# Narrower buffer waits between two layers: waits by tile, page buffers at the far end of memory, five blocks loaded ahead

## The chip, the cores and the metric

The kernel runs on one core of one Trainium2 chip. Its engines each work through their own queue of instructions: TensorE (PE, with its weight loads as PEld) multiplies, VectorE (DVE) and ScalarE (ACT) do elementwise work, GpSimd (POOL) here mostly issues indirect transfers (gathers and scatters by a list of rows), and SyncE (SP) issues plain transfers. The metric is the device time of the kernel in microseconds; the number that counts is the median of several runs.

## The reference, cut to what matters

The input x is 128 graphs of 64 nodes with 256 features, 8192 rows ("tokens") in all. Two layers follow each other, and each has a graph part and a mixture of experts:

```python
# layer 0
x = x + L0_gnn(layernorm(x), adj)          # adj @ x, W1 to 1024, rmsnorm, silu, W2 back to 256
x = x + L0_ffn(layernorm(x))               # below
# layer 1
x = x + L1_gnn(layernorm(x), adj)          # layer norm, adj @ h @ W_rel + h @ W_root, relu, residual
x = x + L1_ffn(layernorm(x))               # 8 experts, top 2, hidden width 512

def L0_ffn(x):                             # 64 experts, top 6
    top_logits, indices = top_k(x @ gate_w.T, 6)
    scores = softmax(top_logits)
    xW = einsum('bsd,bskde->bske', x, lattice_weights[indices])   # a 256x256 matrix per choice
    h = x + einsum('bske,bsk->bse', xW, scores) @ out_w.T + out_b
    return layernorm(h) * ln_g + ln_b
```

All data are float32. Each token has six answers from layer 0's experts, and these six are added up before layer 1 can do anything with the token.

## The kernel before, in words

The kernel has four stages, one after the other.

**Layer 0's blocks** (L579 to L791). 32 blocks of 256 tokens go through the graph part and the gate. `place` works out, for each of a token's six choices, a row in a table in DRAM (`r0x`) that is grouped by expert, and `send` (L314, on POOL) scatters the rows there. When block READY-1 is placed, `look_back` (L169) notes how many rows each expert has by then. After the last block `page_table` (L338) makes a list of pages, 128 rows of one expert each: first the first full pages of every expert (up to R = 3), then the other full pages, then the pages with a rest. `page_table` also works out (L383 to L386) whether the first READY blocks have rows that lie beyond their experts' first full pages; if so, the page count is set so high that the conditional tail of pages runs.

**Layer 0's pages** (L794 to L848). 424 pages, in pairs: `fetch` (L457, on SP) loads a page into one of 46 buffers `px`, `flip` transposes it (L817, L819), `apply` multiplies it by its expert's matrix in `lat` (L831) and by the scores (L836, into `px` again), and `reply` (L321, on POOL) scatters the 128 answers out of `px` to `r0y`, ordered by token. 23 more pages stand in a conditional tail (L845); whether they run is read from the page table. The replies of pages 192 (R times 64 experts) and up form a group of their own, "r0last".

**Layer 1's blocks** (L852 to L1063). Again 32 blocks, laid out by `staggered` as a software pipeline: step s runs the stages of several blocks, `load3(s+2)`, `mixture(s+1)`, `layer_out(s)`, the convolution of block s-1 and s-2, and `choose1`, `count1`, `place1` of block s-3. `load3` (L884 on SP) loads the 1536 answers of a block into one of two buffers `y`, and the block's `xn1`, `x1` and adjacency; `mixture` (L901) transposes and adds the six answers on TensorE. `place1` sends the rows to layer 1's table (L314 again, now `r1x`). For the first READY blocks `load3` says that the y load need not wait for the "r0last" replies (L886, L887). The order on PE, DVE and ACT is the order of the code (`manual_schedule`, L490); that on SP and POOL is decided by the scheduler when the kernel is built. `load_w2` (L1034) loads the second weights `fw2` of layer 1's experts in the course of this stage.

**Layer 1's pages** (L1066 to L1141). 69 pages of 256 rows: `fetch1` loads a page and its expert's first weights (`px`, `pw`, `pb2`), `flip1`, `up` (L1110) and `down` (L1130) compute, and `add` (L331, on POOL) adds the result into the output.

**Buffers.** SBUF pools are laid out one after the other. `lat` (128 KB per partition, L559) holds first the working data of layer 0's blocks and then all 64 expert matrices; `wx0` with `px` and `pxT` lies behind it during the page stage. When the page stage is over, both are given up, and the pools `keep` (fw2, 32 KB), `wx1` (layer 1's page buffers, about 41 KB), `c3` (constants, about 9 KB) and `work3` (the blocks' working data, about 82 KB) come into their place, in this order. The first instruction that uses a buffer in memory that an earlier pool has given up has to wait for the earlier users of that memory. By default a pool waits for all users of the memory that it takes over, whichever of its tiles is asked for. PSUM pools work in the same way.

Of the kernel before, what the change touches and what calls it, by code (L numbers as in the profile page):

```python
# [18 lines left out]
PSUM = bass.MemoryType.PSUM  # L19
# [452 lines left out]
def two_layer_gnn_moe_kernel(ctx: ExitStack, tc: tile.TileContext, a: dict, out: bass.AP):  # L472
# [12 lines left out]
    KH = H0 // P  # L485
    K0 = 6
    E1, F1, _ = a["L1_ffn_W2"].shape
    READY = 4
    KF = F1 // P
    ctx.enter_context(tc.manual_schedule(engines={ENG.PE, ENG.DVE, ENG.Activation}))  # L490

# [87 lines left out]
    with tc.tile_pool(name="c0", bufs=1) as c0, \  # L579
# [161 lines left out]
        def place(b):  # L741
            B = blocks[b]
            r0.normalize(*B["w"], B["xs"])
            r0.send(r0.places(b, B["hot"]), B["xs"])
            if b == READY - 1:
                r0.look_back()
# [44 lines left out]
            nc.sync.dma_start(out=lat[:, e:e + EB], in_=lat_w[:, e:e + EB])  # L791


    with tc.tile_pool(name="wx0", bufs=3) as wx, \  # L794
            tc.tile_pool(name="pt1", bufs=4, space=PSUM) as pt_pool, \
            tc.tile_pool(name="py1", bufs=4, space=PSUM) as py_pool:
        npair = (r0.pages + 1) // 2
        pairs = [dict() for _ in range(npair)]
        regs = {}

        def fetch(j):
            Q = pairs[j]
            for q in range(2):
                i = 2 * j + q
                if i % 4 == 0:
                    regs["row"] = r0.load(0, i, ENG.SP)
                if i < r0.pages:
                    Q["px", q] = px = wx.tile([P, 1, W], F32, name=f"px{q}", bufs=23)
                    r0.fetch(i, regs["row"][i % 4], px)

        def flip(j):
            Q = pairs[j]
            pt = pt_pool.tile([P, KD, C], F32, name="pt")
            n = min(2, r0.pages - 2 * j)
            for q in range(n):
                for k in range(KD):
                    nc.tensor.transpose(pt[:, k, ts(q, P)], Q["px", q][:, 0, ts(k, P)], ident)  # L817
            Q["xT"] = xT = wx.tile([P, KD, C], F32, name="pxT", bufs=5)
            nc.scalar.copy(xT[:, :, :n * P], pt[:, :, :n * P])  # L819

        def apply(j):
            Q = pairs[j]
            if j < E0:
                r0.fill_end(j)
            if j % 2 == 0:
                regs["e"] = r0.load(1, 2 * j, ENG.PE)
            py = py_pool.tile([P, 2, D], F32, name="py")
            n = min(2, r0.pages - 2 * j)
            for q in range(n):
                for k in range(KD):  # L830
                    nc.tensor.matmul(py[:, q, :], lhsT=Q["xT"][:, k, ts(q, P)],  # L831
                                     rhs=lat[:, ds(regs["e"][(2 * j + q) % 4], 1), k, :].rearrange("p o d -> p (o d)"),
                                     start=(k == 0), stop=(k == KD - 1))
            for q in range(n):
                px = Q["px", q]
                nc.vector.tensor_scalar(px[:, 0, :D], py[:, q, :], px[:, 0, D + 1:D + 2], None, op0=ALU.mult)  # L836
                r0.reply(2 * j + q, px[:, 0, :], px[:, 0, :D])


        stages = ((-12, fetch), (0, apply),  # L840
                  (-2, lambda j: flip(j) if j < 4 else None), (-3, lambda j: flip(j) if j >= 4 else None))
        likely = (r0.likely_pages + 3) // 4 * 2
        staggered(likely, stages)
        wait = const.tile([1, 4], F32, name="wait")
        with tc.If(r0.needed(2 * likely)):  # L845
            staggered(npair, stages, likely)

            nc.sync.dma_start(out=wait, in_=r0.answer[0:1, 0:4])  # L848
    lat_pool.__exit__(None, None, None)


    keep = ctx.enter_context(tc.tile_pool(name="keep", bufs=1))  # L852
    fw1 = a["L1_ffn_W1b1"]
    F1W = fw1.shape[2]
    fw2 = keep.tile([P, E1, KF, D], F32, name="fw2")
    wx = ctx.enter_context(tc.tile_pool(name="wx1", bufs=2))
    with tc.tile_pool(name="c3", bufs=1) as c3, \
            tc.tile_pool(name="work3", bufs=2) as work, \
            tc.tile_pool(name="ps3", bufs=3, space=PSUM) as psum, \
            tc.tile_pool(name="po3", bufs=1, space=PSUM) as po_pool, \  # L860
            tc.tile_pool(name="pm3", bufs=1, space=PSUM) as pmix:
        out_wT = load_matrix(c3, "L0_ffn_out_wT")
        ln_g = load_rows(c3, "L0_ffn_ln_g")
        ln_b = load_rows(c3, "L0_ffn_ln_b")
# [15 lines left out]
        def load3(b):  # L880
            B = blocks[b]
            B["y"] = y = work.tile([P, T, K0, D], F32, name="y")
            for t in range(T):
                d = nc.sync.dma_start(out=y[:, t],  # L884
                                      in_=r0.answer[ts(b * T + t, P * K0), :].rearrange("(p k) d -> p k d", k=K0))
                if b < READY:  # L886
                    tc.declare_no_dep(d.ins, group="r0last", reason="in the first pages, or waited for above")  # L887
# [175 lines left out]
        r1.page_table(work.tile([P, 512], F32, name="scratch", bufs=1))  # L1063


    with tc.tile_pool(name="pt4", bufs=2, space=PSUM) as pt_pool, \  # L1066
            tc.tile_pool(name="ph4", bufs=4, space=PSUM) as ph_pool, \
            tc.tile_pool(name="py4", bufs=2, space=PSUM) as py_pool:
        PG = 2 * P
        pages = {i: dict() for i in range(-FIRST, r1.pages)}  # L1070
        regs = {}

        likely = r1.likely_pages - FIRST

        def load1(i, e):
            Q = pages[i]
            Q["w"] = w = wx.tile([P, F1W], F32, name="pw", bufs=3)
            nc.sync.dma_start(out=w, in_=fw1[ds(e, 1)].rearrange("o p f -> p (o f)"))
            Q["b2"] = b2 = wx.tile([P, D], F32, name="pb2", bufs=4)
            nc.sync.dma_start(out=b2, in_=a["L1_ffn_b2"][ds(e, 1), :].to_broadcast([P, D]))  # L1080

        def fetch1(i):
            Q = pages[i]
            Q["x"] = x = wx.tile([P, 2, W], F32, name="px", bufs=4)
            if i < 0:
                if i == -FIRST:
                    regs["first"] = r1.load_first(ENG.SP)
                r1.fetch_first(regs["first"][i + FIRST], x)
                load1(i, i + FIRST)
                return  # L1090
            if i % 4 == 0 or i == likely:
                regs["row"], regs["esp"] = r1.load(0, i, ENG.SP), r1.load(1, i, ENG.SP)
            r1.fetch(i, regs["row"][i % 4], x)
            load1(i, regs["esp"][i % 4])

        def flip1(i):
            Q = pages[i]
            pt = pt_pool.tile([P, KD, PG], F32, name="pt")
            ops.transpose(pt, Q["x"])
            Q["xT"] = xT = wx.tile([P, KD, PG], F32, name="pxT")  # L1100
            nc.scalar.copy(xT, pt)  # L1101

        def up(i):
            Q = pages[i]
            w = Q["w"]
            Q["hid"] = hid = wx.tile([P, KF, PG], F32, name="phid")
            for c in range(KF):
                ph = ph_pool.tile([P, PG], F32, name="ph")
                for k in range(KD):
                    nc.tensor.matmul(ph, lhsT=w[:, k * F1 + c * P:k * F1 + (c + 1) * P], rhs=Q["xT"][:, k, :],  # L1110
                                     start=(k == 0), stop=(k == KD - 1))
                nc.scalar.activation(hid[:, c, :], ph, AF.Relu, bias=w[:, KD * F1 + c:KD * F1 + c + 1], scale=1.0)  # L1112

        def down(i):
            Q = pages[i]
            if 0 <= i < E1:
                r1.fill_end(i)
            if i >= 0 and (i % 4 == 0 or i == likely):
                regs["e"] = r1.load(1, i, ENG.PE)
            e = regs["e"][i % 4] if i >= 0 else i + FIRST  # L1120

            p = wx.tile([P, 2], F32, name="p")
            nc.scalar.activation(p, Q["x"][:, :, D + 1], AF.Exp)  # L1123
            nc.vector.tensor_scalar(p, p, 1.0, None, op0=ALU.add)  # L1124
            nc.vector.reciprocal(p, p)
            py = py_pool.tile([P, 2, D], F32, name="py")
            y = wx.tile([P, 2, D], F32, name="py_s")
            for t in range(2):
                for c in range(KF):
                    nc.tensor.matmul(py[:, t, :], lhsT=Q["hid"][:, c, ts(t, P)],  # L1130
                                     rhs=fw2[:, ds(e, 1), c, :].rearrange("p o d -> p (o d)"),
                                     start=(c == 0), stop=(c == KF - 1))
            nc.vector.tensor_add(y, py, Q["b2"].unsqueeze(1).to_broadcast([P, 2, D]))  # L1133
            for t in range(2):
                nc.vector.tensor_scalar(y[:, t, :], y[:, t, :], p[:, t:t + 1], None, op0=ALU.mult)
                r1.add(i, Q["x"][:, t, :], y[:, t, :])

        stages = (-2, fetch1), (0, flip1), (1, down), (0, up)
        staggered(likely, stages, -FIRST)
        with tc.If(r1.needed(likely)):  # L1140
            staggered(r1.pages, stages, likely)  # L1141
# [32 lines left out]
```

## Time and profile before

| | us |
|---|---|
| median of 10 runs | 2133.24 (2131.16 to 2136.42) |
| profiled execution, its own time | 2136.48 |
| span of the profiled execution | 2134.60 |
| layer 0's blocks, until the last TensorE work of the stage | about 0 to 627 |
| layer 0's pages on TensorE | 662.4 to 1163.5 |
| replies on POOL | 669.7 to 1214.8 |
| layer 1's blocks on TensorE | 1221.2 to 1606.4 |
| layer 1's pages on TensorE | 1606.4 to the end |

The times of all lines in this document count from the start of the span. In the page's slices each digit is the busy share of 53.4 us in tenths. A line of the timeline gives the start, the busy time, the engine (SPq and ACTq are queues that issue transfers), the line of the kernel, the operation, its output and input, how many instructions are grouped, and in brackets the idle time before with what ended it. A line of the waits gives the sum of a wait, how often it occurred, and the longest. TensorE is busy in 1934.1 us of the span (91%), VectorE in 1190.3, ScalarE in 1019.6, GpSimd in 1164.8; the granted TensorE clock was 0.962 of full speed on average.

### The profile page before, as it was taken

The numbers are of one execution on the slowest core, as the hardware profiler recorded it, in microseconds if no ns is written. First come the engines' busy times: TensorE is split into PE (matmuls) and PEld (weight loads), VectorE is DVE, ScalarE is ACT, GpSimd is POOL, SyncE is SP. The second block draws the span as 40 slices with busy tenths as digits, with TensorE's granted clock in tenths as the row PEclk, the third lists the DMA queues.
The fourth block names the chain that finished last, engine by engine and source line by source line (L and its number), as shares of the span: only waits on it lengthen the run. The fifth ranks groups of instructions, "written<-read, shape, count | busy, mean of one in ns | idle before, by whom it ended". The sixth has DMA issues, their size and how long they took to land. (4 is left out here: it accounts for less than half of the span.)

```text
span 2134.6 us, 37458 instructions
## 1 busy us (share of the span) xinstructions
PE 1934.1 (91%) x10564; PEld 1680.8 (79%) x10564; DVE 1190.3 (56%) x3975; ACT 1019.6 (48%) x2037; POOL 1164.8 (55%) x1142
## 2 busy tenths in 40 slices
PE   6999999999945899999997199999989999999997
PEld 5888888888835778888876088888878888888886
DVE  5889899899883333434332078888873222222221
ACT  5888788888831222222221056666653333333332
POOL 1376666666675777777777503333344444444444
PEclk9999999999967999999999599999999999999998
DMA  4244455554377998767775289888835776667765
GB/s 119 93 138 145 151 165 165 165 159 135 121 244 222 301 265 240 209 208 207 209 206 167 95 295 325 266 267 277 259 110 136 181 165 156 158 157 165 167 159 105
DMA packets 284095, 398.97 MB, mean 187 GB/s; under 512 B 56536, under 2 KB 237928, under 8 KB 283888
## 3 DMA queue, kind: packets, MB, share of 16 engines
q1 hardware_dynamic: 204032, 247.67, 40.3%
q0 software_dynamic: 64800, 136.14, 21.3%
q10 hardware_dynamic: 15056, 12.69, 1.8%
q8 instruction: 94, 1.54, 0.3%
q14 instruction: 113, 0.93, 0.2%
HBM read 223.89 MB, written 177.69 MB: 188 GB/s over the span
## 5 line engine op out<-in xcount | busy, mean ns | idle before, releaser
L314 POOL DMA_INDIRECT r0x<-xs,r0row x384 | 394.3, 1027 | 255.9 <-issue 167.7
L321 POOL DMA_INDIRECT r0y<-px x424 | 412.0, 972 | 145.5 <-issue 48.2
L831 PE MATMUL py<-lat,pxT 128*128 x1696 | 406.6, 383 | 20.0 <-ACT pxT L819 15.1
L331 POOL DMA_INDIRECT out_x<-py_s,px x138 | 215.4, 1561 | 300.5 <-DMA out_x<-py_s,px 242.4
L836 DVE TENSOR_SCALAR px<-py,px 128x256 f32<-128x256 f32 x424 | 185.8, 479 | 330.1 <-PE py L831 307.6
L831 PEld LDWEIGHTS py<-lat,pxT 128*128 128x128 f32 x1696 | 306.8, 191 | 62.8 <-ACT pxT L819 20.3
L819 ACT COPY pxT<-pt 128x512 f32<-128x512 f32 x212 | 124.0, 586 | 409.5 <-PE pt L817 275.0
L1112 ACT ACTIVATE phid<-ph,pw 128x256 f32<-128x256 f32 x276 | 130.9, 474 | 323.4 <-PE ph L1110 167.5
L1110 PE MATMUL ph<-pxT,pw 128*128 128x256 f32 x1104 | 251.0, 381 | 0.7 <-ACT pxT L1101 0.7
L1130 PE MATMUL py<-fw,phid 128*128 (+1 forms) x1104 | 250.0, 379 | 0.1
L659 PE MATMUL ph<-lat 128*128 128x256 f32 x1024 | 233.2, 387 | 10.9 <-DVE lat L681 10.2
L692 PE MATMUL ps<-lat 128*128 128x256 f32 x1024 | 237.9, 381 | 0.0
L1110 PEld LDWEIGHTS ph<-pxT,pw 128*128 128x128 f32 x1104 | 210.7, 191 | 30.0 <-ACT pxT L1101 1.1
L659 PEld LDWEIGHTS ph<-lat 128*128 128x128 f32 x1024 | 195.3, 193 | 39.4 <-DVE lat L681 9.9
L1130 PEld LDWEIGHTS py<-fw,phid 128*128 128x128 f32 x1104 | 204.4, 190 | 25.9 <-ACT phid L1112 0.5
L692 PEld LDWEIGHTS ps<-lat 128*128 128x128 f32 x1024 | 193.3, 191 | 24.8
L314 POOL DMA_INDIRECT r1x<-xs,r1row x128 | 130.2, 1017 | 111.8 <-DVE bn_rs L949 56.0
L817 PE MATMUL pt<-ident,px 128*128 128x128 f32 x848 | 132.4, 276 | 39.4 <-DMA px<-r0x 38.8
L817 PEld LDWEIGHTS pt<-ident,px 128*128 128x128 f32 x848 | 106.0, 142 | 66.2 <-issue 36.8
L901 PE MATMUL ps<-ident,y 128*128 128x128 f32 x768 | 92.1, 278 | 57.6 <-DMA y<-r0y 57.6
L1133 DVE TENSOR_TENSOR py_s<-py,pb 128x512 f32<-128x512 f32 x69 | 47.7, 691 | 160.3 <-PE py L1130 147.5
L1124 DVE TENSOR_SCALAR p<-p 128x2 f32<-128x2 f32 x69 | 11.7, 170 | 223.9 <-ACT p L1123 223.9
(282 smaller groups left out, 2880.8 us busy)
## 6 DMA issues: line engine op xcount, KB each, us to landing
px<-r0x SPq DMA_DIRECT2D x424, 129.0 KB
y<-r0y SPq DMA_DIRECT2D x64, 768.0 KB
pw<-in_L_ffn_W1b SPq DMA_DIRECT2D x69, 514.0 KB
px<-r1x SPq DMA_DIRECT2D x69, 258.0 KB
x<-x SPq DMA_DIRECT2D x64, 256.0 KB
pb<-in_L_ffn_b SPq DMA_DIRECT2D x69, 128.0 KB
r0x<-r0filler ACTq DMA_DIRECT2D x64, 129.0 KB
lat<-in_x SPq DMA_DIRECT2D x32, 256.0 KB
```

Of the source, the lines that this page charges most:

```text
L314: i = self.nc.gpsimd.indirect_dma_start(out=self.table[:, :], out_offset=bass.IndirectOffsetOnAxis(ap=row[:, t, k:k + 1], axis=0), in_=xs[ ...
L321: d = self.nc.gpsimd.indirect_dma_start(out=self.answer[:, :], out_offset=bass.IndirectOffsetOnAxis(ap=x[:, self.D:self.D + 1].bitcast(I32 ...
L331: i, d = f"{self.name}add{i}", self.nc.gpsimd.indirect_dma_start(out=self.total[:, :], out_offset=bass.IndirectOffsetOnAxis(ap=x[:, self.D ...
L659: nc.tensor.matmul(ph[:, c, :], lhsT=w1[:, k, ts(2 * j + c, P)], rhs=B["aggT"][:, k, :], start=(k == 0), stop=(k == KD - 1))
L692: nc.tensor.matmul(B["po"][:, t, :], lhsT=B["hT"][:, c, ts(t, P)], rhs=w2[:, c, :], start=False, stop=(t == T - 1 and c == KH - 1))
L817: nc.tensor.transpose(pt[:, k, ts(q, P)], Q["px", q][:, 0, ts(k, P)], ident)
L819: nc.scalar.copy(xT[:, :, :n * P], pt[:, :, :n * P])
L831: nc.tensor.matmul(py[:, q, :], lhsT=Q["xT"][:, k, ts(q, P)], rhs=lat[:, ds(regs["e"][(2 * j + q) % 4], 1), k, :].rearrange("p o d -> p (o ...
L836: nc.vector.tensor_scalar(px[:, 0, :D], py[:, q, :], px[:, 0, D + 1:D + 2], None, op0=ALU.mult)
L1110: nc.tensor.matmul(ph, lhsT=w[:, k * F1 + c * P:k * F1 + (c + 1) * P], rhs=Q["xT"][:, k, :], start=(k == 0), stop=(k == KD - 1))
L1112: nc.scalar.activation(hid[:, c, :], ph, AF.Relu, bias=w[:, KD * F1 + c:KD * F1 + c + 1], scale=1.0)
L1130: nc.tensor.matmul(py[:, t, :], lhsT=Q["hid"][:, c, ts(t, P)], rhs=fw2[:, ds(e, 1), c, :].rearrange("p o d -> p (o d)"), start=(c == 0), s ...
```

## The change

All pools from layer 0's pages on get `reuse_waits="tile"`: the first user of a tile waits only for the earlier users of that tile's own bytes. The pool `wx1` is allocated from the other end of SBUF (`side="right"`), so that `c3` and `work3` move down behind `keep`. READY goes from 4 to 5: `look_back` is taken one block later, and one more block's y load is declared independent of the "r0last" replies.

```diff
-    READY = 4
+    READY = 5
...
-    with tc.tile_pool(name="wx0", bufs=3) as wx, \
-            tc.tile_pool(name="pt1", bufs=4, space=PSUM) as pt_pool, \
-            tc.tile_pool(name="py1", bufs=4, space=PSUM) as py_pool:
+    with tc.tile_pool(name="wx0", bufs=3, reuse_waits="tile") as wx, \
+            tc.tile_pool(name="pt1", bufs=4, space=PSUM, reuse_waits="tile") as pt_pool, \
+            tc.tile_pool(name="py1", bufs=4, space=PSUM, reuse_waits="tile") as py_pool:
...
-    keep = ctx.enter_context(tc.tile_pool(name="keep", bufs=1))
+    keep = ctx.enter_context(tc.tile_pool(name="keep", bufs=1, reuse_waits="tile"))
...
-    wx = ctx.enter_context(tc.tile_pool(name="wx1", bufs=2))
-    with tc.tile_pool(name="c3", bufs=1) as c3, \
-            tc.tile_pool(name="work3", bufs=2) as work, \
-            tc.tile_pool(name="ps3", bufs=3, space=PSUM) as psum, \
+    wx = ctx.enter_context(tc.tile_pool(name="wx1", bufs=2, side="right", reuse_waits="tile"))
+    with tc.tile_pool(name="c3", bufs=1, reuse_waits="tile") as c3, \
+            tc.tile_pool(name="work3", bufs=2, reuse_waits="tile") as work, \
+            tc.tile_pool(name="ps3", bufs=3, space=PSUM, reuse_waits="tile") as psum, \
...
```

The pools po3, pm3, pt4, ph4 and py4 (PSUM) get the same argument. As built, the instructions on PE and POOL keep their order and their number. On DVE, L169 moves one block later. On SP, the scheduler puts the first two loads of fw2 behind the y loads of blocks 0 to 5 instead of ahead of block 0's, and the loads of layer 1's first page weights come a block or so later in the queue; its other transfers keep their order.

More of the change, by code (lines that the diff above doesn't have):

```diff
@@ L855, in two_layer_gnn_moe_kernel @@
     fw2 = keep.tile([P, E1, KF, D], F32, name="fw2")
-    wx = ctx.enter_context(tc.tile_pool(name="wx1", bufs=2))
-    with tc.tile_pool(name="c3", bufs=1) as c3, \
-            tc.tile_pool(name="work3", bufs=2) as work, \
-            tc.tile_pool(name="ps3", bufs=3, space=PSUM) as psum, \
-            tc.tile_pool(name="po3", bufs=1, space=PSUM) as po_pool, \
-            tc.tile_pool(name="pm3", bufs=1, space=PSUM) as pmix:
+    wx = ctx.enter_context(tc.tile_pool(name="wx1", bufs=2, side="right", reuse_waits="tile"))
+    with tc.tile_pool(name="c3", bufs=1, reuse_waits="tile") as c3, \
+            tc.tile_pool(name="work3", bufs=2, reuse_waits="tile") as work, \
+            tc.tile_pool(name="ps3", bufs=3, space=PSUM, reuse_waits="tile") as psum, \
+            tc.tile_pool(name="po3", bufs=1, space=PSUM, reuse_waits="tile") as po_pool, \
+            tc.tile_pool(name="pm3", bufs=1, space=PSUM, reuse_waits="tile") as pmix:
         out_wT = load_matrix(c3, "L0_ffn_out_wT")
@@ L1063, in two_layer_gnn_moe_kernel @@
         r1.page_table(work.tile([P, 512], F32, name="scratch", bufs=1))
-    with tc.tile_pool(name="pt4", bufs=2, space=PSUM) as pt_pool, \
-            tc.tile_pool(name="ph4", bufs=4, space=PSUM) as ph_pool, \
-            tc.tile_pool(name="py4", bufs=2, space=PSUM) as py_pool:
+    with tc.tile_pool(name="pt4", bufs=2, space=PSUM, reuse_waits="tile") as pt_pool, \
+            tc.tile_pool(name="ph4", bufs=4, space=PSUM, reuse_waits="tile") as ph_pool, \
+            tc.tile_pool(name="py4", bufs=2, space=PSUM, reuse_waits="tile") as py_pool:
         PG = 2 * P
```

## The prediction

> **What bounds the kernel now.** I read the page's slices first, to find where TensorE is not busy, then the waits of that stretch, the timeline of the queues that end them, and last the timeline of the stage behind it.
>
> Slices of 53.4 us: PE stands at 9 nearly everywhere, and falls to 1 in slice 22, where DMA is at 2 as well.
>
> ```profile
> PE   6999999999945899999997199999989999999997
> POOL 1376666666675777777777503333344444444444
> DMA  4244455554377998767775289888835776667765
> ```
>
> The waits between 1163 and 1222 us: one gap of 57.6 us, put down to the load of layer 0's answers (y).
>
> ```profile
> PE ps L901 <- DMA y<-r0y: 57.6, 1, 57.6
> DVE r_L_ffn_bg L872 <- DMA r_L_ffn_bias<-in_L_ffn_bias: 11.5, 1, 11.5
> POOL r0y L321 <- DMA r0y<-px: 8.2, 16, 3.7
> ```
>
> The timeline there. SP is free at 1163.65: it issues two loads of fw2, then nothing until 1216.37. POOL issues replies (L321) at an even pace all that time; the y load leaves 2.56 us after the last one.
>
> ```profile
> 1163.65 0.95 SPq L1034 DMA_DIRECT2D fw<-in_L_ffn_W  x2
> ...
> 1207.89 0.97 POOL L321 DMA_INDIRECT r0y<-px  x1 [0.30 <-issue]
> 1209.17 0.97 POOL L321 DMA_INDIRECT r0y<-px  x1 [0.30 <-issue]
> 1213.81 0.97 POOL L321 DMA_INDIRECT r0y<-px  x1 [3.67 <-DMA r0y<-px]
> 1216.37 0.81 SPq L884 DMA_DIRECT2D y<-r0y  x2
> 1216.80 0.61 POOL L275 TENSOR_SCALAR xs<-r1dest 128x4 int32<-128x4 f32 x3 [2.02 <-DMA r0y<-px]
> ```
>
> So the gap is POOL's backlog: 424 replies at 1.277 us from 669.70, against TensorE's 1.08 a page. Blocks 0 to 3 are declared free of the late replies, and yet the first y load waits for all: its bytes come from pools that the replies still read.
>
> Behind it TensorE sets the pace, without gaps:
>
> ```profile
> 1221.17 4.85 PE L901 MATMUL ps<-ident,y 128*128 128x128 f32 x24 [57.65 <-DMA y<-r0y]
> 1228.57 2.78 PE L901 MATMUL ps<-ident,y 128*128 128x128 f32 x24
> 1233.92 2.78 PE L901 MATMUL ps<-ident,y 128*128 128x128 f32 x24
> 1247.69 2.78 PE L901 MATMUL ps<-ident,y 128*128 128x128 f32 x24
> 1258.90 2.82 PE L901 MATMUL ps<-ident,y 128*128 128x128 f32 x24
> 1270.19 2.82 PE L901 MATMUL ps<-ident,y 128*128 128x128 f32 x24
> 1281.48 2.82 PE L901 MATMUL ps<-ident,y 128*128 128x128 f32 x24
> ```
>
> These are the mixtures of blocks 0 to 6; from block 4 on one comes every 11.29 us. Block 5's starts 49.0 us after block 0's.
>
> **Part by part.** *Waits by tile, and wx1 at the other end.* Per partition: keep 32 KB, c3 about 9, work3 about 82; with wx1 (41 KB) moved away that is 124 KB, all within lat's 128. Lat's last user is the matmul that ends at 1163.5, so every buffer of the block stage is free then. In the changed program as built, block 0's y load waits for that matmul and one earlier transfer, no reply; its position on SP is ahead of fw2. It issues at 1163.7 instead of 1216.4.
>
> *READY 5.* Block 4's load is freed too, block 5's is the first that waits for the replies. The two buffers of y are no limit: block 4's load follows block 2's mixture. The condition of L385 now covers 1280 tokens. Counted from the reference on its inputs, the fullest expert has 249 of their rows, and the one nearest its limit (128 times its first full pages, at most 3) is 135 short. So the tail of replies stays out.
>
> *When TensorE is ready for block 5.* The first y took 4.8 us from issue to 1221.17, with the queues to itself; now constants and replies run beside it. I take 1169, and with the old cadence block 5's turn comes at 1169+49=1218. But data may be late: the blocks' start moved 367 GB/s (10.28 MB from 1217 to 1245), and its fullest slices 400 to 430. Replies take 131 KB each 1.277 us, 103 GB/s; of 400 some 300 are left. Up to the end of block 2's y there are 3x1.57+4x0.26 MB and 1.0 of constants, 6.8 MB: 22.6 us and 1.3 of start, so 1187.6, while the old cadence would use the second half at about 1183. That makes 1222.5. Bounds 1217.5 and 1225.
>
> *When block 5's y is there.* The POOL chain starts some 0.7 us earlier: the first reply waited to 669.70, though its DVE product was done at 668.9 (L836), and in the changed program it no longer waits for all queues. Against that, the last 39 replies now run beside VectorE and y loads. The nearest row is the sends of layer 1, with VectorE busy 286.40 of 328 us and DMA at 0.81:
>
> ```profile
> 1281.55 1.03 POOL L314 DMA_INDIRECT r1x<-xs,r1row  x1 [0.53 <-POOL xs L275]
> 1282.88 0.98 POOL L314 DMA_INDIRECT r1x<-xs,r1row  x1 [0.30 <-issue]
> 1284.17 0.97 POOL L314 DMA_INDIRECT r1x<-xs,r1row  x1 [0.30 <-issue]
> 1285.44 0.97 POOL L314 DMA_INDIRECT r1x<-xs,r1row  x1 [0.30 <-issue]
> 1292.61 0.22 POOL L275 TENSOR_SCALAR xs<-r1dest 128x4 int32<-128x4 f32 x1 [6.20 <-DMA r1x<-xs,r1row]
> ```
>
> Their pace is 1.297, so 39 x 0.02 = 0.8 us. The two cancel: y(5) issues at 1216.4, lands 4.8 later, at 1221.2, and up to 1 us more for sends beside it. TensorE's readiness and the data so meet at about 1222.5.
>
> The Trainium skill, "SBUF — State Buffer", section "SBUF: two separate sides", speaks against this: it says that VectorE in a two-port mode locks POOL out, so that descriptors of POOL's transfers can't be written meanwhile. By it the replies would slip by whole VectorE operations; the pace of 1.297 under a VectorE 87% busy does not show that, so the sum keeps 0.8 us.
>
> *The restart.* TensorE idles up to 4 us before block 5. After the 4.9 us gap at 594 the next 29 matmuls took 2.3 us more than their twins 14 us earlier, and mixture 0 took 4.85 for 2.8: 0 to 2.1 us, I take 1.2.
>
> *Free edits.* SP now issues fw2's first two loads within the block stage: 512 KB each, needed only by L1130, first run at 1613; uncovered they would cost 1.3 us each. Behind block 5's waiting y load on SP stand loads of blocks 5 and 6, an output of block 1 and fw2: none is due before block 5's mixture. On POOL, the tags of blocks 0 to 2 and block 0's sends stand behind the replies; block 0's rows come only at the end of step 3 (1269.15 before, some 1217 to 1221 now), when POOL is free. PSUM by tile and the right-hand buffers for layer 1's pages change waits that were long met: 0, at most 1 us. The transition at 625 to 662 stays: the page fetch needs the last send (656.33) itself.
>
> *The sum.* Block 5's mixture goes from 1270.19 to 1222.5: 47.7 us; less 1.2: 46.5. All behind it is TensorE at its own pace to the end, so it shifts as a whole. The profiled execution took 2136.48 (span 2134.60), so 2090.0; it lies 3.24 over the median, which becomes 2086.7. Its own range: mixture 5 between 1220 and 1226, restart 0 to 2.1, so 42 to 50 us, 2083 to 2091.
>
> **Rivals.** *Replies starve.* Four sends beside the block loads took from 1281.55 to 1292.61, 11.1 us with one landing; if that is throughput (2.8 us each), then in the 27 us of block loads 9.6 replies get through instead of 21.1, and 11.5 x 1.277 = 14.7 us are added to POOL's end: gain 33, 2100. For it: the landing, and the slices at 400 GB/s. Against it: the gap before L275 also holds some 2.5 us of plain landing, and POOL's pace held at 1.277 while fw2 and constants filled the queues from 1166 to 1174. The skill's "DMA: Bandwidth & Descriptors", section "Queues, rings and completion order", has each engine turn from queue to queue packet by packet, by which POOL's queue would keep its share. Chance 0.14.
>
> *VectorE holds POOL.* If each of the last 39 replies waits for one VectorE operation of the blocks (L933, 0.47 us), POOL ends 39 x 0.47 = 18 us later: gain 29, 2104. The sends above kept 1.297 beside the same operations: 0.02. It is the rule of the SBUF page as a mechanism of this kernel.
>
> *Only four blocks run ahead* (block 4 finds no data or no buffer in time): mixture 4 then starts at 1221, before 1258.90: gain 37, 2096. Chance 0.04.
>
> *A wait is left.* Some first instruction on ACT or VectorE still hangs on the replies: the y data are there, yet the gap stays, less the 4.8 us of y's landing: 2128. The built program's waits speak against it. 0.02.
>
> *Slower: the tail runs.* If an expert's share of the first five blocks passed its first full pages, L385 would force the conditional pages: 23 more replies at 1.277 = 29 us on POOL, and all y loads behind them: 2163. It decides at 128 rows a full page; by the count, 135 rows away. 0.01; for causes not thought of, 0.02 more on this side.
>
> **How the numbers follow.** The forecast has 0.75. Its range, stretched over the four-block case and the better half of starvation, is 2082 to 2097. Within 0.2% (4 us, about what a measurement here can tell) lies nothing likely: 0.02. Faster 0.95, slower 0.03.
>
> **What would show it.** SP: y at 1163 to 1164, ahead of fw2. PE: mixture 0 near 1169, a gap of 0 to 4 us at mixture 5, then 11.29 us a block. POOL: last reply within 1212 to 1216, replies at 1.28 to 1.30. Starvation would show as a reply pace over 1.4 between 1164 and 1192; a late first VectorE operation as mixture 2 long after 1190. The page stages must keep their lengths; if they do not, the sum was incomplete.

## The result, and the profile after

| | us |
|---|---|
| before, 28 runs | 2133.37 (2128.08 to 2137.48) |
| changed, 8 runs | 2090.15 (2086.55 to 2095.84) |
| ratio | 0.98, 95% interval 0.979 to 0.981 |
| profiled execution of the changed kernel | 2087.06, span 2085.3 |

The changed kernel is 43 us faster by the medians. A second set on another chip (e10 below) gave 2087.53 beside 2136.51, a ratio of 0.9782 (0.9758 to 0.9807). The forecast of 2086.7 lies 3.5 us under the first median, inside its range of 2082 to 2097. The profiled execution of the kernel before took 3.1 us more than its median, that of the changed kernel 3.1 us less than its own, so the two profiles differ by some 6 us more than the medians do.

The slices of the changed kernel, now 52.1 us each: the 1 in PE's slice 22 has become a 7, and DMA's 2 there a 7.

```profile
PE   6999999999973898999999799999979999999997
POOL 1376666666675777777777743433443444444444
DMA  4244555454375998767776779878726766666665
```

The waits between 1160 and 1225 us (engine, line and what it waited for: sum, number, longest). TensorE's 57.6 us for y in one piece are now 11.4 us in five, all of them in blocks 0 to 2.

```profile
DVE r_L_ffn_bg L872 <- DMA r_L_ffn_bias<-in_L_ffn_bias: 14.4, 1, 14.4
...
PE ps L901 <- DMA y<-r0y: 11.4, 5, 5.1
```

The timeline there: SP's first y load, ahead of fw2, mixture 0, and much later the last reply, the y load of block 5, and the mixtures of blocks 4 to 6.

```profile
1162.55 0.81 SPq L884 DMA_DIRECT2D y<-r0y  x2
...
1167.54 2.79 PE L901 MATMUL ps<-ident,y 128*128 128x128 f32 x12 [5.11 <-DMA y<-r0y]
...
1211.16 2.82 PE L901 MATMUL ps<-ident,y 128*128 128x128 f32 x24
...
1213.33 0.97 POOL L321 DMA_INDIRECT r0y<-px  x1 [3.65 <-DVE r1hot L209]
...
1215.57 0.81 SPq L884 DMA_DIRECT2D y<-r0y  x2
...
1222.45 2.82 PE L901 MATMUL ps<-ident,y 128*128 128x128 f32 x24
...
1233.74 2.82 PE L901 MATMUL ps<-ident,y 128*128 128x128 f32 x24
```

POOL's replies end where they ended before (1213.33 against 1213.81), but the mixtures of blocks 0 to 4 now run beside them. Block 5's y load leaves SP at 1215.57 and is there before TensorE wants it: no idle time stands at 1222.45, and the mixtures are 11.29 us apart. Mixture 5 moved from 1270.19 to 1222.45, 47.7 us; the spans differ by 49.3.

What the start of the stage costs is seen in SP's own waits, between 1160 and 1235 us. Block 0's xn load (L889) stands 8.2 us behind a constant that ScalarE's queue had issued at 1163.04; in the built program the two transfers share a completion semaphore (it gives eight of them in turn to the transfers of both queues, and xn is the eighth behind that constant). Block 1's y load, behind it on SP, so leaves only at 1173.21, and mixture 1 waits for it.

```profile
SPq L884 <- DMA r0y<-px: 13.0, 1, 13.0
SPq L889 <- DMA r_L_ffn_ln_g<-in_L_ffn_ln_g: 8.2, 1, 8.2
```

```profile
1171.61 0.37 SPq L889 DMA_DIRECT2D xn<-xn  x1
...
1173.21 0.95 SPq L884 DMA_DIRECT2D y<-r0y  x2
...
1180.55 1.50 PE L901 MATMUL ps<-ident,y 128*128 128x128 f32 x12 [3.45 <-DMA y<-r0y]
```

VectorE's wait of 14.4 us above (L872, the sum of two bias rows) is the other thing that a late constant holds up. It cost at most 0.9 us: the sum starts at 1177.75, VectorE's first work on block 0 at 1178.00, and the matmuls that this work needs end at 1177.09. The next step of block 0, on ScalarE, starts only at 1186.66, behind its copy of block 1's answers (1184.76), so the 0.9 us are not what sets the pace.

### The profile page after: what moved, and what is told of

Its sections match the earlier page's. It is cut to its first block, busy times and chain, and to the rows that moved or that the text cites. A ratio compares the mean times of both kernels' runs of the same rounds, so it can differ in the third digit from the quotient of the medians.

```text
span 2085.3 us, 37427 instructions
## 1 busy us (share of the span) xinstructions
PE 1933.2 (93%) x10564; PEld 1681.1 (81%) x10564; DVE 1188.0 (57%) x3975; ACT 1018.4 (49%) x2037; POOL 1163.4 (56%) x1142
## 5 line engine op out<-in xcount | busy, mean ns | idle before, releaser
L1133 DVE TENSOR_TENSOR py_s<-py,pb 128x512 f32<-128x512 f32 x69 | 47.7, 691 | 156.4 <-PE py L1130 154.2
L683 ACT ACTIVATE lat<-lat,c_L_gnn_rms_weight 128x256 f32<-128x256 f32 x256 | 105.6, 495 | 36.9 <-DVE lat L681 36.4
```

## The experiments

All times are medians; the ratio is to the kernel before on the same chip. The last three columns are from the profiled execution: the start of block 0's mixture, from there to block 6's mixture, and from that to the end of the span.

| | edit | us | ratio, 95% | mixture 0 | 0 to 6 | 6 to end |
|---|---|---|---|---|---|---|
| before | | 2133.37 | | 1221.17 | 60.31 | 853.1 |
| changed | | 2090.15 | 0.98 (0.979 to 0.981) | 1167.54 | 66.20 | 851.6 |
| e1 | before, READY 5 | 2134.38 | 0.9999 (0.9988 to 1.001) | 1223.46 | 59.02 | 852.7 |
| e2 | e1, wx1 right | 2090.70 | 0.9808 (0.9786 to 0.983) | 1166.91 | 66.94 | 852.0 |
| e3 | changed, READY 4 | 2101.15 | 0.9853 (0.9835 to 0.987) | 1166.85 | 77.37 | 853.1 |
| e4 | changed, wx1 left | 2110.89 | 0.989 (0.987 to 0.991) | 1177.03 | 82.81 | 851.5 |
| e5 | changed, READY 6 | 2093.03 | 0.9796 (0.9777 to 0.9814) | 1172.41 | 68.50 | 852.5 |
| e6 | changed, constants in order | 2087.49 | 0.9776 (0.9759 to 0.9794) | 1166.61 | 64.42 | 852.3 |
| e7 | e6, READY 6 | 2082.87 | 0.9757 (0.9738 to 0.9776) | 1166.66 | 61.17 | 849.6 |
| e8 | e7 without waits by tile | 2082.93 | 0.9758 (0.9736 to 0.9779) | 1169.33 | 60.95 | 850.9 |
| e9 | e7, constants by ScalarE | 2083.81 | 0.9762 (0.9741 to 0.9783) | 1166.10 | 63.56 | 849.8 |
| e10 | changed, again | 2087.53 | 0.9782 (0.9758 to 0.9807) | 1168.02 | 68.51 | 849.3 |

The last column is the same in all twelve within 3.8 us, and the changed kernel alone has 851.6 once and 849.3 once. So what the edits do happens ahead of mixture 6.

### Which edit frees the first load: e1, e2, e4

e1 is the kernel before with one edit:

```diff
-    READY = 4
+    READY = 5
```

> The kernel before with READY = 5 and nothing else. Theory (the first y load waits because its bytes were those of buffers that late replies still read, so freeing one more block from the replies is worth nothing by itself): the gap of TensorE ahead of mixture 0 stays at 57 to 58 us, y(0) leaves SP 2 to 3 us after the last reply, 2133 us, as before. Rival (the READY edit carries the gain, the pools only tidy up): y(0) leaves near 1164, 2096 us or less.

Measured: 2134.38 us, ratio 0.9999. The waits keep the gap, and the timeline has the y load 2.56 us after the last reply at 1216.05:

```profile
PE ps L901 <- DMA y<-r0y: 57.3, 1, 57.3
```

```profile
1216.05 0.97 POOL L321 DMA_INDIRECT r0y<-px  x1 [3.66 <-DMA r0y<-px]
1218.61 0.81 SPq L884 DMA_DIRECT2D y<-r0y  x2
```

READY alone is worth nothing. What held the load is shown by the next run: the memory under its buffer, not the rows that it reads.

e2 adds one argument to that, and leaves all pools at their wide waits:

```diff
-    READY = 4
+    READY = 5
...
-    wx = ctx.enter_context(tc.tile_pool(name="wx1", bufs=2))
+    wx = ctx.enter_context(tc.tile_pool(name="wx1", bufs=2, side="right"))
```

> The kernel before with READY = 5 and layer 1's page buffers (wx1) on the right-hand side, but no pool waits by tile. Theory (what frees the loads is where the bytes lie: without wx1 all pools of the block stage lie inside lat's old bytes, whose last user is TensorE): y(0) leaves SP near 1163.5, mixture 5 starts 54 to 56 us after mixture 0, 2090 us, within 4 us of the changed kernel. Rival (the waits by tile carry it): the gap of 57 us stays, 2133 us.

Measured: 2090.70 us, the whole gain. Its timeline has y at 1161.70 and mixture 5 at 1222.56, 55.65 us after mixture 0:

```profile
1161.70 0.81 SPq L884 DMA_DIRECT2D y<-r0y  x2
...
1222.56 2.82 PE L901 MATMUL ps<-ident,y 128*128 128x128 f32 x24
```

With wx1 out of the way, keep, c3 and work3 lie inside lat's 128 KB, and lat's users are done when the page stage ends on TensorE. A wide wait on the right memory costs nothing.

e4 is the other half, waits by tile and READY 5 with wx1 where it was:

```diff
-    wx = ctx.enter_context(tc.tile_pool(name="wx1", bufs=2, side="right", reuse_waits="tile"))
+    wx = ctx.enter_context(tc.tile_pool(name="wx1", bufs=2, reuse_waits="tile"))
```

> The changed kernel with wx1 left at its old place: waits by tile and READY = 5 stay. Theory: the y loads find buffers whose late replies are few, so the first blocks start early; but some buffers of the block stage (s, hT, z, x3) then lie over the px buffers whose last replies are at about 1198 to 1211, and ScalarE's s of block 0 waits for them, about 16 us of stall: gain about 30 of 43 us, 2104 us (2098 to 2112). Rival 1 (the side is irrelevant, waits by tile are enough): 2090 us. Rival 2 (the side is everything): 2133 us.

Measured: 2110.89 us, inside the 2098 to 2112 that was allowed, 7 us over the value named. The timeline shows both things that it pays:

```profile
1168.97 4.46 SPq L884 DMA_DIRECT2D y<-r0y  x2
...
1211.15 0.97 POOL L321 DMA_INDIRECT r0y<-px  x1 [0.30 <-issue]
...
1215.15 1.09 ACT L956 ACTIVATE s<-x,bn_nm,bn_rs 128x256 f32<-128x256 f32 x2 [18.39 <-DMA r0y<-px]
...
1226.05 2.78 PE L901 MATMUL ps<-ident,y 128*128 128x128 f32 x24
```

fw2's first load is back ahead of block 0's y, which leaves at 1168.97 and takes 4.46 us to issue (it waits for constants, among others). That was not expected, but it is covered by what comes next: ScalarE's s of block 0 lies over a buffer of late replies and starts at 1215.15, against 1191.99 in the changed kernel. The bracket puts 18.39 us of idle time down to the replies. My 16 us counted to the issue of a late reply; a buffer is free only when its reply has landed, and the last one issued before s starts left at 1211.15, 4.0 us earlier. Mixture 3, which stands behind s, starts at 1226.05 instead of 1199.95: 26.1 us lost, 21.6 of the 47.7 kept. Tile by tile is a partial remedy here, the place is the whole one.

### Whether the late replies still bind: e3, e5

```diff
-    READY = 5
+    READY = 4        # e3; 6 in e5
```

> The changed kernel with READY back at 4, so that block 4's y load is the first that waits for all replies. Theory: replies still end near 1213.3, y(4) leaves at 1215.6 and lands near 1220.4, so mixture 4, at 1211.2 in the changed kernel, comes 9.2 us later, with up to 1 us of restart: 2100 us (2098 to 2102). Rival (late block data set the pace up to mixture 5 in any case): 2090 us.

Measured: 2101.15 us, 11 us over the changed kernel. Its timeline:

```profile
1212.64 0.97 POOL L321 DMA_INDIRECT r0y<-px  x1 [3.64 <-DMA r0y<-px]
1214.85 0.81 SPq L884 DMA_DIRECT2D y<-r0y  x2
...
1219.29 5.17 PE L901 MATMUL ps<-ident,y 128*128 128x128 f32 x24 [6.63 <-DMA y<-r0y]
...
1232.93 2.82 PE L901 MATMUL ps<-ident,y 128*128 128x128 f32 x24
```

Block 4's y is now the first behind the replies. Mixture 0 to mixture 4 takes 52.4 us against 43.6, so 8.8 us of waiting; then mixture 4 to 5 takes 13.64 instead of 11.29. After an idle time of 6.63 us TensorE so lost another 2.35 us: 5.17 for 24 matmuls that take 2.82 elsewhere. The clock that TensorE was granted shows it: 0.50 of full speed from 1219.3 to 1223.3, 0.65 to 1224.5, and 1.00 behind that. The two make the 11 us. The fifth block ahead is worth that, but only once the place is right (e1).

> The changed kernel with READY = 6: block 5's y load is freed of the replies too, block 6's is the first that waits. Theory (TensorE already reaches block 5 after its y, without a gap): no difference, 2090 us within 1 us. Rival (the replies still bind block 5): up to 6 us faster, 2084 us.

Measured: 2093.03 us, ratio 0.9796 beside 0.98 and 0.9782 for the changed kernel. No gain: a gain of 6 us against the first set would need 0.977, and the interval begins at 0.9777; a difference of 1 us can't be told. In its profiled execution the whole stage began 5 us late (y at 1167.42), since layer 0's pages ended late: their last matmul starts at 1166.9 instead of 1162.0. I don't take that for an effect of the edit: the program up to there is that of the changed kernel but for where look_back is taken, and in the other kernels whose y load goes ahead of fw2 that load spreads from 1161.28 to 1164.94 as well. With one profile of e5 that is not shown. The spacing of 68.50 equals that of e10.

The last reply came late in this run, after 7.41 us in which POOL was idle, against 3.65 in the changed kernel.

```profile
1219.33 0.97 POOL L321 DMA_INDIRECT r0y<-px  x1 [7.41 <-DVE r1top L204]
```

Block 5's y load now runs beside it (SP issues it at 1209.94): from 1212 to 1216 the DMA engines are busy all but a few per cent of the time, where they stand still in the changed kernel. That fits a last reply that waits for earlier ones to land among the loads, but no run separates it. Here it costs nothing, as blocks 0 to 5 no longer wait for that reply.

### What the start loses: e6, e7, e9

Mixtures 0 to 6 take 66.2 to 68.5 us in the changed kernel, 60.3 in the kernel before. e6 and e7 move the constants (ten loads; the expectation miscounted them as eleven):

```diff
-        out_wT = load_matrix(c3, "L0_ffn_out_wT")      # and nine more, on ScalarE's queue, ahead of block 0
-        nc.vector.tensor_add(bg, bg, gbias)
+        def load_consts(b):                            # called in load3, behind block b's y
+            s = nc.sync                                # e9: nc.scalar
+            if b == 0:
+                cn["out_wT"] = load_matrix(c3, "L0_ffn_out_wT", s)
+            elif b == 1:                               # ln_b, ln_g, gamma, beta
+                cn["ln_b"] = load_rows(c3, "L0_ffn_ln_b", s)
...
+            elif b == 2:                               # w_rel, w_root, wg, bg, bias
+                cn["w_rel"] = load_matrix(c3, "L1_gnn_W_rel", s)
...
+            if b == 0:                                 # in choose1, behind the gate matmul
+                nc.vector.tensor_add(cn["bg"], cn["bg"], cn["gbias"])
```

> The changed kernel with the eleven constants of the block stage taken off ScalarE's queue and issued by SP in order of need, between the loads of blocks 0, 1 and 2; VectorE's add of the two bias rows comes after block 0's gate matmul. Theory (in the changed kernel SP's xn load of block 0 stands 8.2 us behind the landing of a constant, and the stage loses 5.9 us against the old spacing at its start): xn(0) leaves within 2 us of y(0), mixture 5 could come about 4 us earlier, but y(5), which lands near 1220.4, then binds: 0 to 2 us faster, 2088 to 2090 us. Rival (the start is bound by the bytes that the DMA engines can move): no difference, 2090 us.

> The same order of constants with READY = 6, so that y(5) no longer binds. Theory: the spacing of mixtures 0 to 6 shrinks by some 4 us, 2086 us. Rival (bytes bind the start): no difference, 2090 us.

Measured: 2087.49 and 2082.87 us. In e6, mixture 5 is ready early and the replies bind after all:

```profile
1214.35 1.45 SPq L891 DMA_DIRECT2D y<-r0y  x2
...
1218.76 1.50 PE L909 MATMUL ps<-ident,y 128*128 128x128 f32 x12 [1.26 <-DMA y<-r0y]
```

In e7 block 5's y doesn't wait for them, and mixture 6 comes 61.17 us after mixture 0:

```profile
1162.03 0.81 SPq L891 DMA_DIRECT2D y<-r0y  x2
1163.36 1.18 SPq L897 DMA_DIRECT2D xn<-xn  x1
...
1227.83 2.82 PE L909 MATMUL ps<-ident,y 128*128 128x128 f32 x24
```

(L909 is the old L901, L891 the old L884, L897 the old L889.) xn now leaves 1.3 us after y instead of 9.1, and the spacing is 5.0 us shorter than in the changed kernel, 0.9 over the one before. The same bytes are moved, so the bytes alone did not make those 5 us; the order of the transfers and their waits for each other did. The edit changes both at once, and no run separates which constants move first from which transfer waits for which. READY 6, worth nothing in e5, is worth something here: of the 3.25 us (64.42 to 61.17), 2.4 stand at mixtures 5 and 6, which come 12.70 and 12.27 us after the one before in e6 and 11.29 in e7. The rest lies ahead of block 4, where READY changes nothing.

> As e7 (waits by tile, READY = 6, constants in order of need), but the constants are issued by ScalarE's queue between its own instructions. Theory (what counts is that the first block loads and the constants don't wait for each other's landing, not which engine issues): between e7 and the changed kernel, 2083 to 2088 us; SP's xn of block 0 leaves within 3 us of y(0). Rival (issue by SP is what helps, since ScalarE's queue shares landing semaphores with SP's): 2090 us, with SP again several us behind a constant.

Measured: 2083.81 us, spacing 63.56, xn 0.86 us after y.

```profile
1161.28 0.81 SPq L891 DMA_DIRECT2D y<-r0y  x2
1162.14 0.42 SPq L897 DMA_DIRECT2D xn<-xn  x1
```

The order takes the wait away whichever engine issues. 2.4 us in the spacing are left between e9 and e7, and SP still has waits of 4.0 and 4.9 us for a constant and for y; but two profiled executions of the changed kernel itself differ by as much (66.20 and 68.51), and in the medians e7 and e9 can't be told apart. So a part of the engine isn't shown.

### Without any wait by tile: e8, beside e10

e8 is e2 with the constants in order and READY 6, without any wait by tile.

> The kernel before with three edits: wx1 on the right-hand side, the constants issued by SP in order of need, READY = 6; no waits by tile. Theory (the place of wx1 alone frees the loads, the order of the constants takes the start's loss away): as e7, 2083 us within 2 us, about 2.4% under before. Rival (the waits by tile are worth something elsewhere, at the start of layer 0's pages or among layer 1's): 2 to 5 us more, 2085 to 2088 us.

Measured: 2082.93 us, ratio 0.9758, with e7 the fastest of the study: 2.4% under the kernel before, and 7.2 and 4.6 us under the changed kernel's two medians. The intervals of the ratios of e8 and of e10 overlap; that the difference is real rests on the spacing, 60.95 and 61.17 against 66.20 and 68.51. The waits by tile are worth nothing measurable anywhere in this kernel, once wx1 is moved.

> The changed kernel itself, on the same chip as e8 and e9: both theories 2090 us. Its row is for the difference to them.

Measured: 2087.53 us.

## Why the prediction was right, by its steps

- *The first y load*: forecast for 1163.7, ahead of fw2; it left at 1162.55, ahead of fw2. Its reason, the place, is shown by e2. The heading named two edits for it, and only the move of wx1 is needed.
- *Mixture 0 near 1169*: 1167.54.
- *Mixture 5 at 1222.5, since data are late*: 1222.45. That it came within 0.05 us is luck: in e10, the same kernel, mixture 5 starts at 1225.24, 45.0 us earlier than before and not 47.7, still inside the bounds of 1220 to 1226. The size was right and half of its reason wrong. I worked it out from bandwidth, 300 GB/s beside the replies. In fact the start came 1.5 us earlier than I had put it, and the slip against the old cadence was 5.9 us instead of 4.5 (54.9 against 49.0 from mixture 0 to 5); the two errors cancelled. The 103 GB/s that I took off for the replies were too much as well: in the kernel before, POOL's queue moved 1.79 MB from 1162 to 1192 us, 60 GB/s (the pages that come last are those with a rest). With 340 GB/s left, the same working gives a slip of only 2 us (an estimate), so bytes explain a third of the 5.9. Between 1163 and 1222 us the core moved 267 GB/s in the changed kernel and 302 in e7, so the DMA engines had room; e7 recovers 5 us with the same bytes in another order. The step that missed this is "constants and replies run beside it", priced as bytes and not as transfers that wait for one another.
- *Block 5's y*: forecast to issue at 1216.4 and to meet TensorE; it issued at 1215.57 and came before TensorE wanted it. Replies ran at 1.286 us each between 1163.69 and 1208.71 (35 intervals), forecast 1.297, before 1.277. From the last send to the first reply it took 12.72 us against 13.37, the 0.7 us that I had put on the other side. Whether the wait by tile brings this is open: all eight profiled executions with it have 12.35 to 12.75, three without have 13.32 to 13.98, but e8, without it too, has 11.82.
- *The restart, 1.2 us*: 0, as TensorE did not idle ahead of block 5. The term was mis-sized for this kernel, and its bound was short for a longer gap: 2.35 us after 6.63 us idle in e3, where I had allowed 2.1. The changed kernel pays its restart at mixture 0, as the kernel before does.
- *The sum*: 47.7 us for mixture 5, as forecast; 49.3 in the spans and 43.2 and 49.0 in the medians of the two sets. The sum subtracted a difference between profiles from a median, and the medians gained less than the profiles in the first set. The miss of 3.5 us lies within what executions differ by: the first y load alone spreads over 6 us (1161.28 in e9 to 1167.42 in e5) among kernels that do nearly the same up to there. So the 1.2 us of the restart can't be read from the median.
- *Rivals*: the replies did not starve, and VectorE did not hold POOL. Either would have shown as a pace over 1.4; it was 1.286 while VectorE was busy 30.85 of 59 us (1163 to 1222), with most of the DMA's slices from 1162 to 1192 at 9. On the second the Trainium skill ("SBUF — State Buffer", "SBUF: two separate sides") says that VectorE in a two-port mode blocks POOL's descriptors. The trace does not show that as a loss here: one reply took 1.25 us and two 1.03 instead of 0.97, and some 0.4 us in all came of it. On the first the Trainium skill ("DMA: Bandwidth & Descriptors", "Queues, rings and completion order") has each DMA engine take turns between the queues, packet by packet. The trace agrees so far as POOL's queue kept its share: it moved 1.60 MB from 1162 to 1192 us, against 1.79 in the kernel before, while the queues of SP and ScalarE moved 8.26 MB beside it and 2.12 before. The turns themselves no run here shows. *Only four blocks ahead* was priced at 2096; e3, which makes just that, took 2101. The gain of 37 that I had priced is there in the profiles (the spans differ by 37.3 us, with mixture 4 at 1219.29 instead of 1221 and 2.35 us lost in the restart that I had left out); the medians on that chip differ by 33.3. The wait that is left did exist as a possibility: e4 is that case, on ScalarE, at 2111.
- *A wrong reading*: TensorE's pace in layer 0's pages is not 1.08 us a page but 1.18 (424 pages from 662.4 to 1163.5). With 1.08 POOL's backlog would be 84 us (424 times 0.197), not the 50 that the trace shows; nothing in the sum hung on it.

## What to carry to other kernels

When the first instruction of a stage waits for work that it has no data from, look at whose bytes its buffer lies on, before looking at the dependence that was declared: moving one pool (e2) did what freeing the data (e1) could not, and narrower waits without the move did half (e4). Then take the next wait: with the load freed, ten constants loaded at the stage's start ahead of need cost some 5 us of spacing, through their order and the waits that they put on another queue, with the same bytes moved. And a look-ahead of n blocks is worth what it saves only until the next limit, so try its size again after each other edit (READY 6: nothing in e5, 2.4 us in e7).

## What the runs showed that I had not expected

- A transfer on SP waited 8.2 us (8.5 in e10) for a constant that ScalarE's queue had issued 0.5 us after SP's y load, though neither uses the other's data; the two shared a completion semaphore in the built program.
- What a restart of TensorE costs is its granted clock, 0.50 of full speed at first. In the kernel before it was 0.50 from 1221.1 to 1224.5, after the gap of 57.6 us (mixture 0 took 4.85 us for 2.8); in e3 it was 0.50 from 1219.3 to 1223.3, after 6.63 us (5.17 for 2.82). The longer wait did not cost more.
- After 3.5 to 4 us of waiting it went both ways. In the changed kernel the clock was 1.00 in mixture 1 after 3.45 us (1180.55, above); in e10, the same kernel, it was 0.50 from 1182.0 to 1187.5 after 3.83 us:

```profile
1182.10 5.35 PE L901 MATMUL ps<-ident,y 128*128 128x128 f32 x24 [3.83 <-DMA y<-r0y]
```

From mixture 1 to mixture 2 this execution so takes 1.0 us more, of the 2.3 by which the two differ in the spacing. No run here says where the limit lies.
